# A cross-attention kernel whose order of operations becomes a table, with turned probabilities and rests of queries moved in fewer transfers

## The chip, the cores and the metric

The kernel runs on one core of one Trainium2 chip. A core has the matrix engine (PE, with its weight loads PEld), the vector engine (DVE), the scalar engine (ACT), GpSimd (POOL) and the sync engine (SP), which here issues most DMA transfers. The metric is device time in microseconds (us), from launch to the end of the slowest (here the only) core. Lower is better.

## The reference

Two batches of 2048 image rows of 640 attend over 124 text tokens of 384, with 8 heads of 80. A second path ("adapter") takes the last 4 context tokens, lets rows derived from them attend over all 2048 image rows, turns the result into queries again and lets these attend over the 4 tokens. Both results are added and go through the output matrix, a bias and the residual. All is float32.

```python
enc = encoder_hidden_states[:, :end_pos, :]          # 124 text tokens
ca = encoder_hidden_states[:, end_pos:, :]           # 4 adapter tokens
query = hidden_states @ Wq
keyt = enc @ Wk
valt = enc @ Wv
hs = _mha(query, keyt, valt)
ca_q1 = jnp.einsum('btc,th->bch', ca, Wq_ca)
indices = np.linspace(0, CROSS_ATTENTION_DIM - 1, unet_size).astype(np.int64)
ca_q1 = ca_q1[:, indices, :]
ca_hs1 = _mha(ca_q1, residual, residual)
ca_q2 = ca_hs1 @ Wq
ca_k2 = ca @ Wk_ca
ca_v2 = ca @ Wv_ca
ca_hs2 = _mha(ca_q2, ca_k2, ca_v2)
out = hs + ca_hs2
out = out @ Wout + b_out
out = out + residual
```

`_mha` splits into heads, takes softmax(q k / sqrt(80)) v per head and joins the heads again.

## The kernel before

**A planner issues everything.** The class `Desk` holds five engines and a pseudo engine "NONE". The kernel is written as some sixty generators (tasks); each yields operations (`Do`) that name their engine or a choice of engines, the events that they wait for, the buffers that they need and free (`Room`), and a function that emits the instructions. `run` (line 166) looks at all operations that could start, by the planner's own durations, takes the earliest (ties by rank, by a correction per task from the table `RANKS`, and by `change`, which discourages a change of PE's tile shape), and `issue` (line 182) emits its instructions. `pin` (line 199) holds every instruction to program order, so that each engine runs exactly the sequence that the planner chose. This happens when the program is built; the chip sees five fixed sequences with semaphores between them.

**Blocks and units.** The 4096 image rows are cut into 8 blocks of 512 (0 to 3 the first batch, 4 to 7 the second), and for the text attention into 16 units of 256, each with two tiles of 128 rows.

**Each block.** `x_load` (line 1124) fetches x so that DVE can turn it 32 by 32. `yz_block` (line 1527) multiplies it by small matrices for the adapter (tile shape 64*32: 64 rows and 32 columns of PE). `queries` and `queries_fast` (line 1321) compute Q = x Wq with 128*32 instructions (`by_columns`, line 219: four column groups side by side), the latter by a scheme of seven products for eight (names `wq_sums`, `x_sums`). The queries of 80 columns a head are stored as 64 + 16: the last 16 columns of all heads ("rests") are split by `halves_away` (line 1479) into a rounded half and what is left of it, sent to DRAM, and brought back by `rest_back` (line 1499) in another arrangement, one half block of 256 rows at a time. There `away` writes one transfer for both parts, and four transfers read it back into `landing`, two for each copy.

**The adapter.** `adapter(b)` (line 1646) runs for each batch 24 scores operations whose 128x2048 results DVE reduces to maxima (`mx`), then 24 whose results ACT exponentiates (`ea`); their tile shape is 32*128. All 96 use one PSUM buffer of four banks (the room `quad`), so the next one waits until DVE or ACT has read the last. `contract` (line 1768) multiplies `ea` by `y` (tiles `acc`), and `second` (line 1806) ends the path with a table of 384 rows in DRAM (`o2`).

**Each unit.** `text_scores` (line 1951) computes two tiles of scores (tile shape 64*128; main part and rests). `softmax` (line 1979) reduces, exponentiates, divides (`share`, on POOL, DVE or ACT, as the planner finds them free), turns 32 by 32 (`eb`) and sends the result to DRAM (`kept`). `probabilities` (line 2017) brings a unit's probabilities back, turned, as `pT`: keys on partitions, 32 partitions a transfer, four transfers a unit. `text_out_fast` (line 2171) multiplies them by V (`ph`), copies the results out (`hs`, on ACT or DVE), forms their sums (on DVE or POOL) and runs four `chain`s (line 2226) of products with Wout or sums of it, again seven products for eight; after each step of a chain DVE adds the bank's partial result to rows of x (`x_more`, `last_rows`) before the next step adds to the same bank. `stored` (line 2297) lets POOL gather the adapter's rows onto the sum (`add_second`, line 2127) and stores it; the last unit gathers first and stores by halves (`stored_half`).

**Order of keys.** Key c of a head lies in column c of the scores and of the exponentials, whose last four of 128 columns are zero. The 32-by-32 turns cut the columns into four groups j of 32, and in `pT` key 32 j + b lies on partition 32 j + b: a transfer for each j.

Of the kernel before, what the change touches and what calls it, by code (L numbers as in the profile page):

```python
# [59 lines left out]
class Task:  # L60
    def __init__(self, gen, rank, key, more):
        self.gen, self.rank, self.key, self.more, self.last = gen, rank, key, more, Event()


class Desk:
# [4 lines left out]
    WHOLE, SWITCH, LEAVE, ANOTHER = (P, P), 328.5, 9.9, 185.7  # L70
    START = {(P, P): 0.107, (64, P): 0.143, (P, 64): 0.107, (64, 32): 0.1, (P, 32): 0.03}
    DRAIN = {
        ((P, P), (32, P)): 0.136, ((P, P), (64, P)): 0.035, ((P, P), (P, 64)): 0.056, ((P, P), (P, 32)): 0.067,
        ((32, P), (P, 32)): 0.049, ((P, 64), (P, P)): 0.07, ((P, P), (P, P)): 0.0,
    }
    DRAINS = {(64, P): 0.172, (32, P): 0.108, (P, 32): 0.115}
    MORE = {
        "v_transpose": 0.025, "v_stream_shuffle": 0.09, "v_scalar_tensor_tensor": 0.07, "v_reciprocal": 0.035,
        "a_activation": 0.045,
    }  # L80
    COLD = 5.2
    TAIL = {"PE": 0.25, "DVE": 0.18, "ACT": 0.2, "POOL": 0.25, "SP": 0.1, "NONE": 0.0}


    RANKS = {
        "adapter": {0: 1, 1: 2},
        "chain": {2: 8, 4: -11, 5: 7, 6: -2, 8: -11, 11: -4, 14: 11, 15: 16, 19: -14, 24: -4, 25: 3, 30: 3.1,
            32: 4, 34: 10, 36: 2, 41: 0.5, 42: 1, 43: 0.5, 44: -10, 45: -10, 48: -8, 50: -5, 51: -5, 52: 7,
            54: 10, 55: 10, 56: 10, 68: -4, 76: -3, 81: 2, 86: 2, 87: 3},
        "contract": {0: 5, 1: 4.5, 2: 8, 3: 8},  # L90
        "halves_away": {1: -4, 2: -2, 4: 4, 6: 6},
        "keys": {0: -10},
        "probabilities": {3: -8, 5: -4, 8: 12, 9: -3, 10: -2, 12: 6, 13: 6, 15: 7},
        "queries_fast": {0: 5, 3: 4},
        "rest_back": {1: 11, 4: 5, 7: 8, 9: 9, 10: 5, 14: 2},
        "second": {0: 2.3},
        "softmax": {0: 5, 2: -7, 3: 6.2, 4: -4, 7: -11, 8: 2, 10: -5, 12: -20, 14: -3, 17: 9, 20: -2, 21: 7,
            22: 7, 25: -5, 29: 2, 30: 6},
        "sums_of_wq": {0: 5.7},
        "text_scores": {0: -8, 1: 3.4, 12: 9},  # L100
        "values_weights": {0: -18},
        "x_load": {1: 4.2, 4: 5},
        "y_rows": {2: 2, 3: 6, 4: 4},
        "y_weights": {0: 1},
        "yz_block": {2: 16, 5: 3.5, 6: 5},
    }

    def __init__(self, tc):
        self.tc, self.nc, self.now, self.spent, self.mode = tc, tc.nc, 0.0, 0.0, None
        self.free = {e: 0.0 for e in self.ENGINES}  # L110
        self.queue = {e: [] for e in self.ENGINES}
        self.events, self.landed, self.channel, self.log, self.begun = {}, 0.0, 0.0, [], {}

# [6 lines left out]
    def begin(self, gen, rank):  # L120
        name = gen.__name__
        n = self.begun[name] = self.begun.get(name, -1) + 1
        task = Task(gen, rank, (name, n), self.RANKS.get(name, {}).get(n, 0.0))
        task.last.t = self.now
        self.go_on(task, None)

    def go_on(self, task, value):
        while True:
# [7 lines left out]
        op.task, op.at = task, Event()  # L136
# [5 lines left out]

    def change(self, mode):


        if mode is None or mode == self.mode:
            return 0.0
        return self.LEAVE if self.mode == self.WHOLE else self.SWITCH if mode == self.WHOLE else self.ANOTHER

    def order(self, op):  # L150
        return (op.order() if callable(op.order) else op.order) + op.task.more
# [14 lines left out]
    def run(self):  # L166
# [105 lines left out]
def kernel(  # L272
# [1174 lines left out]

    def front_rooms():

# [940 lines left out]
```

## Time and profile before

| what | value |
|---|---|
| time, median of 3 runs | 581.55 us (581.11 to 582.66) |
| the profiled execution | 581.8 us |
| its span, first to last instruction | 580.1 us |
| granted clock of PE | 1.000 |
| DMA packets | 153039, 112.71 MB |
| SP transfers of `pT<-kept`, of `kept<-eb` | 64, 32 |

The span is what the profile's rows divide up; the run's time has 1.7 us more around it. In rows of groups, the columns after the bar are busy time, the mean of one in ns, and the engine's idle time just before them with what ended it. `128*32` is the tile shape, rows by columns of PE; a float32 product shows as two passes, and by_columns' four groups run side by side, so eight records make one product. A row of the timeline has start, length, engine, line, operation, names and count; in square brackets the idle time before it and what ended it. Nearly all emitting lines are helpers of the planner (L210 `matmul`, L222 `by_columns`, L230 `transpose`, L245 vector, scalar and GpSimd operations, L265 `dma`), so groups are told apart by names. Idle time of an engine that is not the bottleneck costs nothing.

### The profile page before, as it was taken

How to read it: one execution, taken by the hardware profiler on the slowest of the kernel's cores; microseconds unless marked ns; L12 is line 12 of the kernel's file. 1: busy time of each engine (PE TensorE's matmuls, PEld its weight loads, DVE VectorE, ACT ScalarE, POOL GpSimd, SP SyncE). 2: the span in 40 equal slices, each digit the busy share in tenths (PEclk: the TensorE clock that was granted, in tenths of full speed). 3: DMA queues.
4: the chain of work that ended last, by engine and by line, in shares of the span. 5: the costliest groups of instructions: out<-in, count | busy, mean ns of one | idle time of the engine just before them, and what ended most of it. 6: DMA issues, size and time to landing. Idle time of an engine off the chain costs nothing.

```text
span 580.1 us, 19105 instructions
## 1 busy us (share of the span) xinstructions
PE 570.3 (98%) x8115; PEld 308.4 (53%) x8115; DVE 391.7 (68%) x645; ACT 309.8 (53%) x869; POOL 141.6 (24%) x200
## 2 busy tenths in 40 slices
PE   9999999999999999999999999999999999999997
PEld 8885334555555545455455445454455545545453
DVE  2446799999999756356999999973455253444443
ACT  2413376686566898689847447277877613002020
POOL 9102112012206411120114326050140312403241
PEclk9999999999999999999999999999999999999999
DMA  8897866979766888234999969999549487799995
GB/s 245 196 263 131 199 94 187 179 201 172 182 184 137 217 157 221 82 113 149 219 284 247 230 152 236 270 227 275 142 105 266 112 211 155 181 263 247 250 249 139
DMA packets 153039, 112.71 MB, mean 194 GB/s; under 512 B 83701, under 2 KB 126581, under 8 KB 152954
## 3 DMA queue, kind: packets, MB, share of 16 engines
q1 hardware_dynamic: 147322, 100.80, 67.5%
q0 software_dynamic: 5632, 10.69, 11.3%
q8 instruction: 64, 1.05, 0.8%
q14 instruction: 21, 0.17, 0.1%
HBM read 71.23 MB, written 40.22 MB: 192 GB/s over the span
## 4 chain that ended last, share of the span: by engine, by line
PE 64%; DVE 16%; DMA 8%; ACT 6%; issue 4%; SPq 1%; DVEq 0%; ACTq 0%
PE po L222 25%; PE pq L222 9%; PE ph L210 6%; DVE mx L245 6%; PE acc L210 5%; PE s L210 4%; PE pq L210 4%; PE sc L210 3%; ACT ea L245 3%; DMA kept<-eb 3%; DMA pT<-kept 2%; ACT p L245 2%; DVE m L245 2%; DVE q L245 2%; DVE eb L245 2%
## 5 line engine op out<-in xcount | busy, mean ns | idle before, releaser
L245 DVE TENSOR_REDUCE mx<-s 128x4 f32<-128x2048 f32 x48 | 109.4, 2280 | 4.1 <-PE s L210 4.1
L245 ACT ACTIVATE ea<-s 128x2048 f32<-128x2048 f32 x48 | 91.0, 1897 | 24.2 <-PE s L210 23.9
L245 ACT ACTIVATE p<-sc,m 128x124 f32<-128x124 f32 x256 | 90.2, 383 | 10.2 <-DVE m L245 9.7
L222 PE MATMUL po<-wout_sums,hs 128*32 128x320 f32 x1024 | 77.3, 433 | 0.0
L222 PE MATMUL po<-wout_sb,hs 128*32 128x320 f32 x960 | 74.2, 433 | 0.7 <-DVE x_more L245 0.7
L222 PE MATMUL pq<-xt,wq_sb 128*32 128x256 f32 (+1 forms) x928 | 66.3, 418 | 0.5 <-DVE mt L245 0.5
L245 DVE TENSOR_TENSOR x_more<-x_more,po 128x320 f32<-128x320 f32 x72 | 34.3, 483 | 45.5 <-PE po L222 45.4
L2129 POOL DMA_INDIRECT x_more<-o,query x18 | 27.9, 1550 | 124.3 <-DVE x_more L245 92.5
L245 ACT ACTIVATION_READ_ACCUMULATOR p<-sc,m 128x1 f32 x256 | 57.8, 226 | 0.0
L245 ACT COPY hs<-ph 128x512 f32<-128x512 f32 (+1 forms) x34 | 18.5, 551 | 65.8 <-PE ph L210 65.2
L222 PEld LDWEIGHTS po<-wout_sums,hs 128*32 128x32 f32 x1024 | 32.9, 110 | 34.1 <-issue 1.8
L210 PE MATMUL acc<-ea,y_sb 128*32 128x384 f32 (+2 forms) x768 | 51.0, 385 | 0.0
L222 PEld LDWEIGHTS po<-wout_sb,hs 128*32 128x32 f32 x960 | 30.4, 110 | 33.1 <-issue 1.5
L245 DVE TENSOR_REDUCE m<-sc 128x4 f32<-128x496 f32 x64 | 40.0, 662 | 10.4 <-PE sc L210 10.4
L245 DVE TENSOR_TENSOR last_rows<-last_rows,po 128x320 f32<-128x320 f32 x56 | 26.7, 481 | 27.9 <-PE po L222 27.5
L210 PE MATMUL ph<-pT,vpad 128*32 128x256 f32 x768 | 45.3, 380 | 0.1
L245 POOL TENSOR_TENSOR p<-p,r 128x992 f32<-128x992 f32 x8 | 14.8, 1846 | 125.0 <-DVE r L245 125.0
L222 PEld LDWEIGHTS pq<-xt,wq_sb 128*32 128x32 f32 x928 | 27.8, 109 | 29.6 <-issue 13.5
L245 DVE STREAM_TRANSPOSE eb<-p 128x1024 f32<-128x1024 f32 x32 | 39.4, 1233 | 5.6 <-DMA kept<-eb 5.5
L210 PEld LDWEIGHTS sc<-kmain,q 64*128 64x128 f32 x512 | 32.1, 187 | 13.7 <-issue 5.5
L210 PE MATMUL sc<-kmain,q 64*128 64x124 f32 x512 | 38.4, 285 | 0.2 <-ACT p L245 0.2
L245 ACT CAST rests<-landing 128x512 fp32r<-128x512 f32 x30 | 18.7, 635 | 36.2 <-PE sc L210 28.0
(216 smaller groups left out, 847.6 us busy)
## 6 DMA issues: line engine op xcount, KB each, us to landing
kept<-eb SPq DMA_DIRECT2D x32, 512.0 KB, 3.8
pT<-kept SPq DMA_DIRECT2D x64, 256.0 KB, 8.2
landing<-away SPq DMA_DIRECT2D x60, 128.0 KB, 4.3
xi<-in_x_dram SPq DMA_DIRECT2D x56, 128.0 KB, 4.6
x_more<-in_x_dram SPq DMA_DIRECT2D x18, 320.0 KB, 6.8
out_dram<-x_more SPq DMA_DIRECT2D x16, 320.0 KB, 6.6
last_rows<-in_x_dram SPq DMA_DIRECT2D x14, 320.0 KB, 7.2
out_dram<-last_rows SPq DMA_DIRECT2D x14, 320.0 KB, 10.0
```

Source lines behind the costliest of these rows:

```text
L210: self.pin(self.nc.tensor.matmul(out, lhsT, rhs, **kw))
L222: self.pin(self.nc.tensor.matmul(out[j : j + 32], lhsT[:, j : j + 32], rhs, **kw))
L245: self.pin(getattr(engine, what)(*args, **kw))
L2129: desk.pin(nc.gpsimd.indirect_dma_start(out=t, out_offset=None, in_=o2_of[b], in_offset=bass.IndirectOffsetOnAxis(ap=query[:, st : st + 1] ...
```

## The change

**The order.** `RANKS`, `order` and `change` go; in their place stands `TURNS`, which gives each operation of each task (by the task's path in the tree of forks) one number: its place in the whole order is the number's size, its engine the number modulo six. `run` takes operations in that order. Operations whose engine could be chosen get it from the table. The planner's durations are changed too; they no longer decide the order, but still appear in the code.

```diff
+        ".1": [959], ".2": [38, 53, 54, 72, 84, 96, 102, 114, 126, 156, 162, 186, 198, 216, 354, 936], ".3": [362],
...
     def run(self):
+        turn = lambda op: self.TURNS[op.task.path][op.num]
         while any(self.queue.values()):
-            best = None
-            for e in self.ENGINES:
-                found = [(max(r, self.free[e], self.now), op) for op in self.queue[e] if (r := self.ready(op)) is not None]
-                if found:
-                    t = min(x[0] for x in found)
-                    t, op = min(
-                        (x for x in found if x[0] <= t + 1e-9),
-                        key=lambda x: self.order(x[1]) + self.change(x[1].mode),
-                    )
-                    if best is None or t < best[0]:
-                        best = t, e, op
-            assert best, [(e, [(op.order, op.fn.__qualname__) for op in q]) for e, q in self.queue.items()]
-            self.issue(*best)
+            op = min((op for q in self.queue.values() for op in q), key=turn)
+            engine = self.ENGINES[turn(op) % len(self.ENGINES)]
+            self.issue(max(self.ready(op), self.free[engine], self.now), engine, op)
```

**Bookkeeping that follows from it.** Buffers are freed by operations of "NONE" that wait for all their users (`free_x`, `free_q`), where counters decided before; `stored` waits for all sums of a tile by name, always gathers, and has no branch through DRAM; `residual` of the last unit waits for the adapter's table. These emit no instructions.

**Turned probabilities.** Keys take another place in the scores: key 4 k + j lies in column 31 j + k. ACT writes each head's 124 exponentials as four runs of 31 with a zero column after each (`et`), so that after the turns key 4 b + j is row b of group j, and the four transfers of a unit become one over all 128 partitions.

```diff
-        et = e[:, :, :NK]
+        et = e.rearrange("p h (j k) -> p h j k", j=4)[:, :, :, : NK // 4]
...
-                            et[:, h, :], s4[u][:, j, :], AF.Exp, bias=less[u][:, j : j + 1],
+                            et[:, h], s4[u][:, j, :].rearrange("p (j k) -> p j k", j=4), AF.Exp, bias=less[u][:, j : j + 1],
...
-        by_keys = kept.rearrange("(i b) j n -> j b i n", i=4)
+        by_keys = kept.rearrange("(i b) j n -> (b j) i n", i=4)
...
-        for j in range(4):
-            op = yield Do(
-                "SP",
-                lambda: dma(pT[R * j : R * (j + 1)].rearrange("p i k h a -> p i (k h a)"), by_keys[j], 1.1),
-                [("kept", m, 0), ("kept", m, 1)], rank=0,
-            )
+        op = yield Do(
+            "SP", lambda: dma(pT.rearrange("p i k h a -> p i (k h a)"), by_keys, 2.8, 0.38),
+            [("kept", m, 0), ("kept", m, 1)], rank=0,
+        )
...
-                pk3 = pk[:, : B * NTOK].rearrange("p (b t) -> p b t", b=B)[:, :, :NK]
+                pk3 = pk[:, : B * NTOK].rearrange("p (b k j) -> p b j k", b=B, j=4)[:, :, :, : NK // 4]
```

**Rests of queries.** The 16-column rests are laid out so that a row of DRAM holds all four groups of one column. The two parts of a half block go out in a transfer each, as soon as each is there, and come back in one transfer of 4 KB runs, whose source is read twice (a stride of 0). The keys' rests follow the same arrangement once, with four transfers out and one back.

```diff
-        away = away_of[n] = hbm.tile([P, 2, 512], F32, tag=f"rest_{n}", name=f"away_{n}")
+        away = away_of[n] = hbm.tile([2, R, 2, 8 * P], F32, tag=f"rest_{n}", name=f"away_{n}")
...
+            def part_away(i, k=k, z=z):
+                dma(away[k, :, i].rearrange("q (g n) -> q g n", g=4), z[:, i].bitcast(F32), 0.45, 0.45)
...
+            for i, at_i in enumerate((main_at, op.at)):
+                yield Fork(one(Do(
+                    "SP", lambda i=i, part_away=part_away: part_away(i), [at_i], marks=[both_away[i]], rank=0,
+                )), 1)
...
-        for u in range(2):
-            by_rows = away_of[n][VH * u : VH * (u + 1)].rearrange("(g d) i n -> (d i) g n", g=4)
-            for e in range(2):
-                yield Do(
-                    "SP",
-                    lambda u=u, e=e, by_rows=by_rows: dma(
-                        t[VH * u + G * e : VH * u + G * (e + 1)], by_rows[:, :, 2 * P * k : 2 * P * (k + 1)], 0.7
-                    ),
-                    [op.at], marks=[("landed", m, u, e)], rank=0,
-                )
+        by_rows = away_of[n][k].rearrange("q i n -> (q i) n").unsqueeze(1).to_broadcast([2 * R, 2, 8 * P])
+        yield Do(
+            "SP", lambda: dma(t.rearrange("p g n -> p (g n)"), by_rows, 1.45, 0.5), [op.at], marks=[("landed", m)],
+            rank=0,
+        )
```

The columns of the last piece of Wq are put in the matching order (`columns`), and a small mask for the adapter's keys is computed for it on DVE (`own`, three short operations in the front).

More of the change, by code (lines that the diff above doesn't have):

```diff
@@ L80 @@
     }
     COLD = 5.2
[L82 to L105, printed above, removed]
@@ L106 @@
+    TAIL = {"PE": 0.235, "DVE": 0.14, "ACT": 0.145, "POOL": 0.16, "SP": 0.1, "NONE": 0.0}
+    TURNS = {
[204 rows of a table added]
     }
@@ L2133, in add_second @@
         ))
-        desk.spent += 1.9
-        desk.landed = desk.now + desk.spent + 6.5
+        desk.transfer("POOL", 1.7, 1.57)
     def text_out(m):
@@ L2266, in chain @@
-                ends.setdefault((m, i), []).append(op.at)
-                if not tile_left[m, i]:
-                    yield Fork(stored(m, i, ends[m, i]), 1)
+        reads = {(i, u): [] for i in range(2) for u in range(2)}
+        for n, steps in enumerate(chains):
+            for _, _, (place,) in steps:
+                reads[place].append(("sum", m, *place, n))
+        yield Fork(one(Do(
+            "NONE", lambda: None, [("chain", m, n) for n in range(len(chains))], frees=[(hss, at_hs)]
+        )), 0)
```

348 lines of the change are left out of this document (174 added, 174 removed), and 203 rows, old and new, of the table TURNS.

## The prediction

> **What bounds the kernel now.** I read the page first, then the windows, then PE's timeline.
>
> ```profile
> span 580.1 us, 19105 instructions
> ...
> PE 570.3 (98%) x8115; PEld 308.4 (53%) x8115; DVE 391.7 (68%) x645; ACT 309.8 (53%) x869; POOL 141.6 (24%) x200
> ...
> PE 64%; DVE 16%; DMA 8%; ACT 6%; issue 4%; SPq 1%; DVEq 0%; ACTq 0%
> ```
>
> TensorE is busy for 98% of the span. The chain of waits runs for a third of its length over other engines, but that matters only where PE goes idle, and PE is idle for 580.1 − 570.3 = 9.8 us in all. The windows say where.
>
> ```profile
> 0.00:20.00 20.00, 18.86 (x113) 17.03 (x114) 6.73 (x41) 5.39 (x10) 15.57 (x59) 1.00 0.90 274
> ...
> 100.00:150.00 50.00, 49.51 (x756) 26.50 (x748) 49.74 (x65) 33.98 (x133) 11.31 (x9) 1.00 0.90 190
> 150.00:200.00 50.00, 49.48 (x774) 27.30 (x772) 43.87 (x59) 33.46 (x113) 14.59 (x21) 1.00 0.67 170
> 200.00:250.00 50.00, 49.41 (x775) 24.97 (x779) 26.53 (x47) 40.82 (x82) 7.50 (x5) 1.00 0.61 153
> 250.00:300.00 50.00, 48.23 (x745) 27.14 (x733) 39.69 (x57) 40.83 (x120) 7.19 (x6) 1.00 0.73 193
> 300.00:350.00 50.00, 48.96 (x714) 24.29 (x706) 48.87 (x52) 25.43 (x99) 16.56 (x15) 1.00 0.89 216
> ...
> 400.00:450.00 50.00, 49.44 (x787) 25.99 (x779) 23.09 (x39) 38.66 (x69) 7.67 (x6) 1.00 0.70 188
> ...
> 550.00:580.00 30.00, 26.38 (x412) 13.41 (x404) 12.11 (x26) 3.09 (x6) 9.24 (x6) 1.00 0.78 194
> ```
>
> The columns after the length are PE, PEld, DVE, ACT and POOL busy, then the clock (1.00 throughout) and DMA. Idle PE: 1.1 in the first window (before the first product), 3.6 in the last (after the last one), and 0.49 + 0.52 + 0.59 + 1.77 + 1.04 + 0.56 = 5.0 in between. So a new order can win little: the products are the same 8115, and what it can remove is those 5.0 us and time that hides inside "busy" PE. Two such kinds show in the timeline.
>
> ```profile
> 400.63 1.26 PE L222 MATMUL po<-wout_sums,hs 128*32 128x320 f32 x16
> 401.70 0.72 PE L222 MATMUL po<-wout_sb,hs 128*32 128x320 f32 x8
> ...
> 407.51 1.26 PE L222 MATMUL po<-wout_sums,hs 128*32 128x320 f32 x16
> 408.70 0.56 PE L210 MATMUL s<-cop,zop 32*128 32x128 f32 x8
> 409.19 1.07 PE L210 MATMUL acc<-ea,y_sb 128*32 128x256 f32 x16
> ```
>
> Sixteen 320-column instructions, four at a time, take 401.70 − 400.63 = 1.07 us when the next ones use the same tile shape (128*32), and 408.70 − 407.51 = 1.19 when adapter scores (32*128) follow: leaving the 128*32 shape costs 0.12. The other kind is waits:
>
> ```profile
> 272.43 0.56 PE L210 MATMUL s<-cop,zop 32*128 32x128 f32 x8 [0.22 <-ACT ea L245]
> ...
> 273.38 1.88 ACT L245 ACTIVATE ea<-s 128x2048 f32<-128x2048 f32 x1 [1.00 <-PE s L210]
> ...
> 275.31 0.51 PE L210 MATMUL s<-zop,cop 32*128 32x512 f32 x4 [0.46 <-ACT ea L245]
> ...
> 285.38 1.92 PE L222 MATMUL pq<-xt,wq 128*32 128x512 f32 x16
> ...
> 285.47 2.28 DVE L245 TENSOR_REDUCE mx<-s 128x4 f32<-128x2048 f32 x1
> ...
> 287.81 0.51 PE L210 MATMUL s<-zop,cop 32*128 32x512 f32 x4 [0.51 <-DVE mx L245]
> ```
>
> All adapter scores share one PSUM buffer of four banks. From one score operation to the next at least 2.88 us pass (275.31 − 272.43) where ACT reads it, and about 3.2 (0.95 from score to reader, then 2.28) where DVE does; less other work than that between two of them makes PE wait. At 285.47 the reader itself started late, behind other DVE work. A recorded wait is longer than it says: the sixteen 512-column products at 285.38 last 1.07 × 512/320 = 1.71, plus 0.12 for the shape, so the scores could have started at 287.21; the wait was 0.60, not 0.51. With some 20 such waits at 0.1 each, I call the removable waiting 5.0 + 2.0 = 7.0 us.
>
> **The change, part by part. The order.** Both kernels pin each engine's program order; the table gives another one. A table entry modulo six is the engine, its size the place. PE has 550 operations in both, the same set. Sorting the table gives 102 departures from the 128*32 shape, against 107 that I count along PE's timeline; departures from the other shapes differ by one at most. That is 5 × 0.12 = −0.6 us. Next the score spacing. Laying the new PE order out with the durations above (scores 0.49, from 408.70 to 409.19, sixteen product instructions 1.07, and so on), 14 of the 96 score operations come sooner than 2.88 or 3.2 after the one before, against 10 in the old order; the shortfalls add up to 4.1 us in both. One is large: between entries 7092 and 7158 stands a single contraction (two passes of 512 columns, 0.86 at the rate above), which leaves 2.88 − 0.49 − 0.86 − 0.12 = 1.4 us short. Some of the small ones vanish because any earlier wait widens the spacing; I take 1.4 + 1.4 = 2.8 us as left. The waits of the old order that have other causes (a late DVE reader, an accumulating bank whose partial sum is still being read) are those that a recalculated order can remove; by the same layout the steps of one accumulation stand far enough apart everywhere but for 0.3 us in all. So 7.0 − 2.8 = 4.2 us go. Bounds: 0, if as many new ones arise, and all 7.0.
>
> **Who does what.** Softmax's division moves among engines.
>
> ```profile
> L245 DVE TENSOR_REDUCE mx<-s 128x4 f32<-128x2048 f32 x48 | 109.4, 2280 | 4.1 <-PE s L210 4.1
> L245 ACT ACTIVATE p<-p,r 128x124 f32<-128x124 f32 x104 | 31.5, 386 | 8.1 <-DVE r L245 8.1
> L245 POOL TENSOR_TENSOR p<-p,r 128x992 f32<-128x992 f32 x8 | 14.8, 1846 | 125.0 <-DVE r L245 125.0
> L245 DVE TENSOR_TENSOR p<-p,r 128x992 f32<-128x992 f32 x11 | 13.6, 1239 | 0.3
> L245 ACT COPY hs<-ph 128x512 f32<-128x512 f32 (+1 forms) x34 | 18.5, 551 | 65.8 <-PE ph L210 65.2
> ```
>
> Of 32 divisions, 8 ran on POOL, 11 on DVE and 104/8 = 13 on ACT; the table puts 20, 3 and 9 there. DVE is relieved of 8 × 1.24 = 9.9 us, but takes 14 more of the copies `hs<-ph` (5 before, 19 now; 0.55 each on ACT, about 8 us), so its 391.7 us stay. POOL takes 12 × 1.85 = 22 us more on 141.6. The result is needed a transfer and many us later, so the slower POOL costs nothing; without that cover it would cost 0.6 each. The activations write the same 124 elements in four runs instead of one; I take 0, and were each 10% slower, ACT (53% busy) would still cover it.
>
> **The transfers.** The turned probabilities come back in one transfer a unit instead of four; the rests of a half block go out in two instead of one and come back in one instead of four.
>
> ```profile
> kept<-eb SPq DMA_DIRECT2D x32, 512.0 KB, 3.8
> pT<-kept SPq DMA_DIRECT2D x64, 256.0 KB, 8.2
> landing<-away SPq DMA_DIRECT2D x60, 128.0 KB, 4.3
> ...
> 309.54 1.84 SPq L265 DMA_DIRECT2D pT<-kept  x4
> ...
> 532.59 5.80 SPq L265 DMA_DIRECT2D pT<-kept  x4
> ```
>
> SP issues 64 − 16 = 48 transfers fewer for the probabilities and 64 + 16 − 16 − 32 = 32 fewer for the rests, at 1.84/4 = 0.46 each some 37 us of its queue; SP is not on PE's path, so this wins nothing by itself. The bytes stay. What matters is whether one transfer of 4 × 256 KB lands before its products. Bounds for its landing: 3.8, what half of it takes as `kept<-eb`, and 14.0, the 5.8 over which one unit's four issues stretched (at 532.59) plus 8.2. I take 8.2, the quarter's median while its siblings are in flight, as the sixteen engines carry the same bytes. In the table the work on PE between that issue and the unit's first product is 8.0 us in the tightest unit (the third; entries 8536 to 8796), then 10.6, 11.7, 11.8, 12.9, and 14 or more in the other eleven. So +0.2 us; at 14.0 it would be 6.0 + 3.4 + 2.3 + 2.2 + 1.1 = 15.0. The rests' single transfer replaces quarters that landed in 4.3, with 4 KB runs instead of 1 KB; 0.
>
> **The ends.** The front keeps its idle 1.1 us and the same loads. The tail:
>
> ```profile
> 567.52 1.54 POOL L2129 DMA_INDIRECT last_rows<-o,query  x1 [0.61 <-DVE last_rows L245]
> ...
> 575.66 0.72 PE L222 MATMUL po<-wout_sb,wout_sums 128*32 128x320 f32 x8
> ...
> 576.45 0.49 DVE L245 TENSOR_TENSOR x_more<-x_more,po 128x320 f32<-128x320 f32 x1 [1.13 <-PE po L222]
> ...
> 576.97 0.33 SPq L265 DMA_DIRECT2D out_dram<-x_more  x1
> ```
>
> After the last product come one addition, one store and its landing, 580.1 − 576.4 = 3.7 us, in both. The last gather-add started 8.9 us before PE's end; in the table 8.6 us of products follow it, and its store stands ahead of the last two half stores on SP's queue, where a late landing would hold them: 0, at most +1.
>
> **The sum.** The profiled execution took 581.8 us, 1.7 beyond its span and 0.25 above the median of the runs. Against the median: 581.55 − 0.6 − 4.2 + 0.2 = 577.0.
>
> **The rivals.** (1) *Nothing is won.* PE is full in both, and the order before was also laid out by a planner; the new one meets other waits of the same size, since DVE is as full (49.74 of 50 in the window 100 to 150) and the score shortfall is equal. Against it: the waits found had causes that an order can avoid. Time: 581.55 − 0.6 = 581.0, no change that can be told. (2) *The single transfer is late: slower.* Landing later than about 12.1 us, its waits (4.1 + 1.5 + 0.4 + 0.3 = 6.3) push 577.0 over 583.3. For it: DMA reads 0.89 and 0.90 busy in two of the windows above, and PE's queue is in order, so one late unit holds everything. Against it: the four, issued within 1.84 at 309.54, took only about 1.84 + 8.2 = 10 in all. With a landing of 13: 5.0 + 2.4 + 1.3 + 1.2 + 0.1 = 10.0, so 587. (3) *POOL's divisions hold DVE.* If each of 12 more divisions kept DVE from its own two-input work for 1.85 us, DVE would gain 22 − 9.9 = 12 us in stretches where it is the fullest engine; half of it on PE's path gives 583. Against it: PE lost only 0.49 us in the window where DVE was busy for 49.74 of 50. The Trainium skill (GPSIMD Engine Reference, Key points) speaks for this one: GpSimd shares its SBUF interfaces with VectorE, contends with instructions of two SBUF inputs, and VectorE does elementwise work about twice as fast. The trace has 1.85 against 1.24 for the division, 1.5 times; whether it held DVE, the group rows do not show.
>
> **How the numbers follow.** Forecast 0.66 (its own range 572.5 to 579.8), rival 1 0.17, rival 2 0.12, rival 3 0.05. About 0.3%, 1.7 us, is what a measurement of this kernel can tell from no change: faster means under 579.8, slower over 583.3. So faster 0.66, same 0.17, slower 0.17. The low end is all 7.0 us gone and the shortfall absorbed, with a little from the tail: 581.55 − 0.6 − 7.0 = 574.0, and 2.5 more for waits that hide deeper in busy PE than I count: 571.5. The high end takes in rival 3 and the near half of rival 2: 585.
>
> **What would show it.** PE's idle time in the windows between 20 and 550 falls from 5.0 us to about 2, with a wait of some 1.4 us on ACT's `ea` just before the last scores of the first batch. The `pT` row shows 16 issues of 1024 KB landing in about 8 us, and no `ph` product names a DMA as what ended its wait; if one does, rival 2 is at work. POOL's `p<-p,r` stands at x20. Rival 3 would show as DVE idle on "issue" and additions of one SBUF pair growing beyond their length. PE's busy time falling by more than 1 us, or a wait over 3 us anywhere, would contradict the account.

## The result: no change that can be told, and the profile after

| kernel | median us (runs) | lowest to highest | standard deviation |
|---|---|---|---|
| before | 581.76 (17) | 580.62 to 582.66 | 0.5 |
| changed | 581.10 (17) | 579.02 to 583.88 | 1.3 |

The ratio is 0.9988, 95% interval 0.9975 to 1.0001. The forecast was 577.0, with 571.5 to 585.0 as its range; the time is that of rival 1 (581.0). The runs of the changed kernel scatter more than twice as much, which no part of the prediction had looked at.

The page of the changed kernel first, its rows as in the prediction.

```profile
span 579.8 us, 18971 instructions
...
PE 566.5 (98%) x8115; PEld 308.3 (53%) x8115; DVE 390.7 (67%) x663; ACT 290.9 (50%) x813; POOL 160.3 (28%) x213
...
L425 POOL TENSOR_TENSOR p<-p,r 128x992 f32<-128x992 f32 x20 | 38.9, 1943 | 169.7 <-DVE r L425 148.8
...
L425 DVE TENSOR_TENSOR x_more<-x_more,po 128x320 f32<-128x320 f32 x64 | 30.5, 482 | 37.6 <-PE po L403 37.3
...
kept<-eb SPq DMA_DIRECT2D x32, 512.0 KB, 4.6
pT<-kept SPq DMA_DIRECT2D x16, 1024.0 KB, 7.6
landing<-away SPq DMA_DIRECT2D x15, 512.0 KB, 4.8
```

The same products take PE 3.8 us less (570.3 before), yet the span shrinks by 0.3. The rest is idle time, so the windows come next (PE, PEld, DVE, ACT, POOL, clock, DMA share, GB/s).

```profile
0.00:20.00 20.00, 18.27 (x107) 16.66 (x108) 7.68 (x34) 3.94 (x7) 15.40 (x59) 1.00 0.86 270
...
100.00:150.00 50.00, 49.24 (x756) 26.21 (x752) 49.67 (x61) 30.23 (x111) 13.78 (x10) 1.00 0.69 157
...
250.00:300.00 50.00, 48.82 (x798) 29.22 (x802) 41.03 (x60) 42.78 (x134) 7.84 (x6) 1.00 0.51 168
...
320.00:340.00 20.00, 19.00 (x289) 10.52 (x284) 18.17 (x23) 14.59 (x57) 0.74 (x1) 1.00 1.02 335
340.00:360.00 20.00, 19.08 (x272) 9.71 (x268) 17.63 (x25) 6.84 (x34) 9.50 (x7) 1.00 0.76 225
...
550.00:580.00 30.00, 22.75 (x340) 10.62 (x332) 11.50 (x26) 0.00 (x0) 13.32 (x9) 0.96 0.80 187
...
565.00:574.00 9.00, 9.00 (x136) 4.16 (x128) 3.08 (x7) 0.00 (x0) 2.82 (x2) 1.00 0.92 245
```

PE is idle for 0.76 + 1.18 + 1.00 + 0.92 us in the four stretches between 100 and 360, and with the rest of the windows for 4.5 us between 20 and 550, against 5.0 before. More is lost outside. In the first 20 us PE idles for 1.73 us, against 1.14 before; the second profile of the same kernel (e1) has 1.13 there, so this loss comes in some runs and not in others. Behind 550 us stands a wait of 1.38 where the old order had none. The rows of that wait and of the end, by PE's timeline:

```profile
555.08 1.28 PE L403 MATMUL po<-wout_sums,hs 128*32 128x320 f32 x16 [1.38 <-POOL hs L425]
...
572.87 1.26 PE L403 MATMUL po<-wout_sb,hs 128*32 128x320 f32 x16
```

It ends at 572.87 + 1.26 = 574.13, where the old order ended at 575.66 + 0.72 = 576.38. So PE is done 2.2 us earlier, but the tail from there to the end of the span grew from 3.7 to 5.7 us. Together these are −3.8 in busy PE, −0.5 + 1.4 in its waits, +1.9 in the tail and +0.6 in the front: −0.4, near the 0.3 by which the spans differ. DMA is at its fullest in one of the stretches where PE idles: share 1.02 and 335 GB/s from 320 to 340. In the stretches from 100 and from 250 its share is only 0.69 and 0.51, so not every wait goes with transfers. The windows of the kernel before for the same two places:

```profile
320.00:340.00 20.00, 19.65 (x280) 9.19 (x276) 19.80 (x23) 7.82 (x33) 4.69 (x7) 1.00 1.04 235
565.00:575.00 10.00, 10.00 (x156) 4.95 (x152) 4.16 (x10) 0.00 (x0) 3.08 (x2) 1.00 0.57 126
```

DMA's share is as high there, but its rate is lower and PE loses 0.35 instead of 1.00; at the end the share is 0.57 instead of 0.92. What PE waited for, in the list of waits (total, times, longest):

```profile
PE po L403 <- POOL hs L425: 2.3, 2, 1.4
PE s L394 <- ACT ea L425: 1.2, 2, 1.0
PE unread L394 <- DVE zeros L425: 1.1, 1, 1.1
PE ph L394 <- DMA pT<-kept: 1.0, 1, 1.0
```

POOL's timeline around the two waits on `hs`, and DVE's longest wait for a landing before `eb`:

```profile
327.25 1.25 DVE L425 STREAM_TRANSPOSE eb<-p 128x1024 f32<-128x1024 f32 x1 [0.67 <-DMA kept<-eb]
...
345.42 2.43 POOL L425 TENSOR_TENSOR p<-p,r 128x992 f32<-128x992 f32 x1
347.22 2.12 POOL L425 TENSOR_TENSOR hs<-hs 128x256 f32<-128x256 f32 x2
...
550.87 1.55 POOL L2323 DMA_INDIRECT last_rows<-o,query  x1 [12.40 <-DMA last_rows<-in_x_dram]
552.73 1.55 POOL L2323 DMA_INDIRECT x_more<-o,query  x1 [0.31 <-issue]
553.70 1.33 POOL L425 TENSOR_TENSOR hs<-hs 128x256 f32<-128x256 f32 x1
```

A sum that a chain needs stands on POOL behind a division (345.42) and, near the end, behind two gathers that waited for a load. And DVE's turn into the only buffer `eb` (327.25) needs the store before it to have landed.

### The profile page after: what moved, and what is told of

The parts are those of the page before. It is cut to its first block, busy times and chain, and to the rows that moved or that the text cites. A ratio compares the mean times of both kernels' runs of the same rounds, so it can differ in the third digit from the quotient of the medians.

```text
span 579.8 us, 18971 instructions
## 1 busy us (share of the span) xinstructions
PE 566.5 (98%) x8115; PEld 308.3 (53%) x8115; DVE 390.7 (67%) x663; ACT 290.9 (50%) x813; POOL 160.3 (28%) x213
## 4 chain that ended last, share of the span: by engine, by line
PE 75%; DMA 7%; DVE 7%; SPq 4%; ACT 2%; issue 2%; POOL 2%; DVEq 0%; ACTq 0%; POOLq 0%
PE po L403 23%; PE pq L403 19%; PE acc L394 7%; PE sc L394 6%; PE ph L394 6%; PE s L394 6%; PE pq L394 3%; SPq L445 3%; DVE mx L425 2%; DMA last_rows<-in_x_dram 2%; PE pyz L394 2%; DMA last_rows<-o,query 2%; DVE xt L425 1%; DMA xi<-in_x_dram 1%; ACT ea L425 1%
## 5 line engine op out<-in xcount | busy, mean ns | idle before, releaser
L425 POOL TENSOR_TENSOR p<-p,r 128x992 f32<-128x992 f32 x20 | 38.9, 1943 | 169.7 <-DVE r L425 148.8
L403 PE MATMUL po<-wout_sums,hs 128*32 128x320 f32 x1024 | 78.7, 433 | 1.4 <-POOL hs L425 1.4
L403 PE MATMUL po<-wout_sb,hs 128*32 128x320 f32 x928 | 72.1, 434 | 1.0 <-POOL hs L425 0.9
L425 DVE TENSOR_TENSOR last_rows<-last_rows,po 128x320 f32<-128x320 f32 x64 | 30.3, 482 | 46.9 <-PE po L403 46.7
L425 ACT ACTIVATION_READ_ACCUMULATOR p<-sc,m 128x1 f32 x256 | 56.4, 220 | 0.0
L425 DVE TENSOR_TENSOR x_more<-x_more,po 128x320 f32<-128x320 f32 x64 | 30.5, 482 | 37.6 <-PE po L403 37.3
L394 PE MATMUL ph<-pT,vpad 128*32 128x256 f32 x768 | 48.0, 380 | 1.0 <-DMA pT<-kept 1.0
L425 POOL TENSOR_TENSOR hs<-hs 128x256 f32<-128x256 f32 x29 | 27.2, 1029 | 71.1 <-ACT hs L425 31.2
L425 ACT COPY hs<-ph 128x512 f32<-128x512 f32 (+1 forms) x24 | 13.6, 573 | 54.2 <-PE ph L394 54.1
L2323 POOL DMA_INDIRECT x_more<-o,query x16 | 25.5, 1593 | 53.0 <-DVE x_more L425 45.5
```

The source lines that it names most:

```text
L394: self.pin(self.nc.tensor.matmul(out, lhsT, rhs, **kw))
L403: self.pin(self.nc.tensor.matmul(out[j : j + 32], lhsT[:, j : j + 32], rhs, **kw))
L425: self.pin(getattr(engine, what)(*args, **kw))
L2323: desk.pin(nc.gpsimd.indirect_dma_start(out=t, out_offset=None, in_=o2_of[b], in_offset=bass.IndirectOffsetOnAxis(ap=query[:, st : st + 1] ...
```

## The experiments

All times are medians; the ratio is to the kernel before, run on the same chip, with its 95% interval. Edits of the order change single entries of the table: task, operation, old place, new place. Tails are measured from the end of PE's last row; the expectations count from the start of the last product, 0.45 us earlier.

**e1, the changed kernel again.**

> The changed kernel once more, unaltered, for a second profile of it. Theory A (the new order removes old waits and makes new ones at fixed places): the same places come back, each within 0.4 us: 1.6 us at unit 8's product before the last gathers' sums (POOL hs), 1.2 at unit 2's first product (DMA pT<-kept), 1.1 before the last scores of the first batch (ACT ea), 1.1 at unit 2's last chain (POOL hs), and 5 to 6 us between PE's end and the last landing; time 581.1. Theory B (the waits are spread at random by DMA landings): other places, the same sum of 4 to 5 us.

Measured: 580.9 (579.33 to 583.45), 0.9979 (0.9966 to 0.9992). Three waits came back at their places (`ea` 1.03, `pT` 1.17, `hs` of unit 2 0.92), so theory A holds for them. The one before the last gathers' sums, expected at 1.6, was 0.47. And in this profile another stands at 378, and behind it a store that took 11.4 us to land (timeline of SP, DVE and PE):

```profile
364.54 0.52 SPq L445 DMA_DIRECT2D kept<-eb  x1
...
376.05 1.25 DVE L425 STREAM_TRANSPOSE eb<-p 128x1024 f32<-128x1024 f32 x1 [1.67 <-DMA kept<-eb]
...
378.12 1.28 PE L403 MATMUL po<-wout_sums,hs 128*32 128x320 f32 x16 [0.71 <-DVE x_more L425]
```

DVE, in order, held an addition to `x_more` behind the turn, and PE waited for the addition. Part of the waiting is a matter of landings, not of places alone.

**e2, new order with four transfers a unit; e3, old order with one.**

```diff
-            "SP", lambda: dma(pT.rearrange("p i k h a -> p i (k h a)"), by_keys, 2.8, 0.38),
+            "SP", lambda: [
+                dma(pT[R * j : R * (j + 1)].rearrange("p i k h a -> p i (k h a)"), by_keys[R * j : R * (j + 1)], 1.1)
+                for j in range(4)
+            ],
```

e3 takes the key layout of the change into the kernel before; its first operation of four issues the whole transfer, the other three nothing.

> The changed kernel with its order, but each unit's turned probabilities come back in four transfers of 32 partitions, issued one behind the other at the place of the single one. Theory A (the order decides): SP's queue is 16 x 1.4 = 22 us busier and the wait at unit 2's first product stays at 1 to 2.5 us; time 581 to 583. Theory C (the single transfer costs what the order won): the DMA wait goes and the time falls by 1.2 us or more, to 580 or less.

> The kernel before with its own order on every engine, instruction for instruction, but with one transfer a unit for the turned probabilities, at the place of the first of the four (keys placed as in the changed kernel). Theory A: within 0.5 us of before, 581.8, since PE's order is the same and its waits are not on these transfers. Theory C: 583 or more, with products ph that wait on DMA pT<-kept. If the shorter queue of SP is worth anything by itself it shows here, as 581 or less.

Measured: e2 591.03, 1.0162 (1.0141 to 1.0183), ten us slower than the changed kernel, which neither theory allowed. e3 581.46, 0.9989 (0.9981 to 0.9998), some 0.7 faster than before. So theory C is wrong both ways round: the single transfer costs neither order anything, and the new order cannot do without it. The 0.7 is as much as the whole change won in the first measurement (0.66). In e2, unit 2's product waited for 4.2 us, as PE's timeline shows:

```profile
337.37 1.94 PE L394 MATMUL ph<-pT,vpad 128*32 128x256 f32 x16 [4.18 <-DMA pT<-kept]
```

The clock fell while PE still waited, and stayed low behind the wait, as e2's windows show (clock third from the end).

```profile
330.00:337.40 7.40, 3.19 (x52) 2.08 (x49) 5.39 (x5) 2.94 (x10) 0.00 (x0) 0.81 1.05 285
337.40:341.00 3.60, 3.60 (x32) 1.75 (x36) 1.89 (x3) 1.58 (x8) 0.74 (x1) 0.50 0.95 266
```

At half the clock the sixteen 256-column instructions above took 1.94 us instead of the 1.07 of the `acc` row in the prediction. Between 20 and 550 PE idles for 10.9 us here, and is busy for 570.3: both rose.

**e4, two waits on POOL taken away.**

```diff
+for path, n, old, new in (
+    ('.71.1', 2, 13215, 13293),
+    ('.71.1', 3, 13245, 13299),
+    ('.58.3.6', 0, 9123, 9122),
+    ('.58.3.7', 0, 9147, 9128),
+):
+    assert Desk.TURNS[path][n] == old
+    Desk.TURNS[path][n] = new
```

> The changed kernel with two sums of unit 2 on DVE instead of POOL and the first two gathers of the last unit behind unit 8's last sum on POOL. Theory A: the two waits on POOL hs (1.6 at 555 us and 1.1 at 349 us) go and nothing takes their place: 581.1 - 2.7 = 578.4. Theory B: the time moves by less than 1 us, and waits of the same size stand elsewhere.

Measured: 581.31 (579.77 to 584.35), 0.9990 (0.9976 to 1.0004): theory B's time. The two waits are gone, and others stand in their place (PE's timeline of e4):

```profile
330.27 0.74 PE L403 MATMUL po<-wout_sb,hs 128*32 128x320 f32 x8 [1.04 <-DVE x_more L425]
335.78 1.07 PE L394 MATMUL ph<-pT,vpad 128*32 128x256 f32 x16 [1.74 <-DMA pT<-kept]
```

The window around them:

```profile
320.00:340.00 20.00, 17.18 (x257) 9.27 (x249) 16.02 (x22) 12.71 (x51) 0.74 (x1) 1.00 0.94 288
```

PE loses 2.8 us here, where the changed kernel's first profile lost 1.0. Both waits lie ahead of the place that was edited, where this kernel's order is that of the changed one. So the edit did not make them. The row at 335.78 names a landing; the one at 330.27 stands behind a turn into `eb` that started 2.20 us late, and that a landing held it is not shown. A profile of one run cannot price an edit here.

**e5 to e8, single places.** e5 moved unit 8's last store behind the last half stores and a chain step of the last unit behind one of unit 8; e6 fetched unit 2's probabilities two places earlier; e7 moved the last adapter scores of the first batch behind the text scores, to fill the 1.4 us that the prediction had found short; e8 has all these and e4's.

```diff
+    ('.64.3.9', 2, 13678, 13732),
+    ('.71.3.13', 0, 13392, 13518),
+    ('.71.3.13', 1, 13454, 13526),
...
+    ('.58.3', 2, 8536, 8506),
+    ('.54.8.1', 0, 8506, 8512),
+    ('.60.1', 1, 8512, 8518),
...
+    ('.55', 108, 7158, 7206),
+    ('.55', 109, 7189, 7207),
+    ('.55.1', 3, 7236, 7290),
+    ('.55.1', 4, 7280, 7292),
+    ('.55.1', 5, 7374, 7428),
+    ('.55.1', 6, 7412, 7436),
```

> The changed kernel with unit 8's gathered store issued behind the last half stores on SP's queue, and one chain step of the last unit behind one of unit 8, on PE and DVE, so that unit 8's last gather starts earlier. Theory A (the order's gain of 2.2 us at PE's end is given back in the tail, 5.7 us from the last product's start to the end of the span against 3.5 to 4.2 before): the tail falls to 4.2 to 4.6 and the time by 1.1 to 1.6, from 581.0 to 579.6. Theory B (the end is set by how many stores are in flight, whatever their order): within 0.5 us of 581.0.

> The changed kernel with unit 2's turned probabilities fetched two places earlier on SP's queue, ahead of one store of x_sums and one of probabilities. Theory A: the wait at unit 2's first product (1.2 and 1.35 us in two profiles) goes, time 579.8. Theory D (the stretch from 320 to 340 us is full of transfers: DMA share 1.00 to 1.02 there in both profiles): what is passed lands later by as much, and the wait stands again at 0.7 us or more, there or at an addition of x_more; time 580.5 to 581.3.

> The changed kernel with the last adapter scores of the first batch behind the text scores that followed them, and the first two of the second batch behind products of queries, on PE, ACT and DVE alike. Theory A: the wait of 1.1 us on ACT's ea at 275 us goes, at most one more change of shape (0.1) comes: 580.0 if it reaches the end. Theory D: PE only runs earlier into the full stretch of transfers behind it, which ends when it ended before: 580.8 to 581.2, with 1 us more waiting between 320 and 400.

> The edits of the four kernels that move single places, together (sums and gathers off POOL's queue, the tail, the earlier transfer of unit 2, the adapter's scores). Theory A: 581.0 - 1.4 - 1.2 - 1.0 - 1.5 = 576 to 577.5, if each stands by itself; the POOL edit alone gave nothing, so without it 577.5 to 578.5. Theory D: only the tail and what lies behind 400 us counts, 579 to 580.

Measured: e5 581.11, 0.9987 (0.9974 to 0.9999). e6 581.94, 0.9996 (0.9979 to 1.0013), in two groups, six runs from 579.76 to 581.01 and six from 582.86 to 583.9. e7 588.42, 1.0103 (1.0077 to 1.0129). e8 588.84, 1.0105 (1.0085 to 1.0124). No edit won anything that can be told, and e7 and e8 lost some 7 us, which no theory allowed. e5's tail was 4.7 us, shorter than in the first two profiles, and its time is theory B's all the same. In e7 the last scores feed exponentials that the contraction behind them needs, so the wait moved there and grew (PE's timeline):

```profile
280.81 1.35 PE L394 MATMUL acc<-ea,y_sb 128*32 128x128 f32 x16 [2.04 <-ACT ea L425]
```

and the clock fell behind it, as e7's windows show:

```profile
282.00:284.00 2.00, 1.97 (x24) 0.89 (x24) 0.00 (x0) 2.00 (x13) 0.00 (x0) 0.50 0.57 222
```

In all PE idles for 9.7 us between 20 and 550 in e7 and is busy for 569.2, against 4.5 and 566.5.

**e9 and e10, fewer transfers in the full stretch.** Both kernels without the same stores; in the old one the order is kept on every engine.

```diff
+            if m in (11, 12, 13):
+                desk.spent += 0.45
+                return
...
+        kept = kept_of[9 if m in (11, 12, 13) else m].rearrange("p j k n -> p j (k n)")
```

> The changed kernel without the stores of the turned probabilities of units 11 to 13, which read unit 9's again: 512 KB less at 314, 320, 328 and 336 us, and the next turn on DVE (one buffer eb) no longer waits for such a store to land. Theory D (the new order puts these transfers so close that the stretch from 320 to 400 is paced by their landings, more or less by chance from run to run): DVE's waits for a landing before eb (0.67 and 0.28 in one profile, 2.20 and 0.95 in the slowest) vanish, PE loses less than 1 us between 320 and 340 instead of 1.0 to 2.8, the time falls to 579 to 579.6 and the runs spread as before's do (standard deviation 0.5 instead of 1.2 to 1.5). Theory A (fixed places of the order alone): 580.7 or more, with the spread unchanged.

> The kernel before with the same stores left out, its order kept, as a control. Theory D: its stores stand 12 us and more apart where DMA is full, so nothing waits for them: 581.7 to 582.2, within 0.5 of before, spread as before's. If any order gains from less to transfer, 580.5 or less.

Measured: e9 579.89, 0.9956 (0.9944 to 0.9968), standard deviation 0.7. e10 582.36, 0.9998 (0.9987 to 1.0009). Against its own chip's before, e9 is 2.5 us faster, the changed kernel 0.7 and 1.35 faster than its own. The stores cost the new order some 1.2 to 1.9 us and the old one nothing; the interval of e9 is clear of the first measurement's and just touches e1's (0.9966 to 0.9992). DVE's waits before `eb` vanished from 300 us on (two earlier ones, at 193 and 218, stayed). Of PE's loss between 320 and 340, 0.9 us stayed:

```profile
320.00:340.00 20.00, 19.08 (x292) 10.54 (x286) 18.50 (x24) 14.59 (x57) 0.73 (x1) 1.00 0.89 267
```

That is a wait on `pT` (0.92), so theory D's time came, with only part of its waits. The edit removes bytes and, with them, the landings that later turns and fetches of the three units wait for; it does not tell the two apart. The old order is not free of such waits either. Its stores from 364 to 394 follow each other by 8.3 to 10.7 us, not 12; in the profile of the prediction a turn into `eb` waits 5.00 us for a landing (404.88), and PE 0.53 for the addition behind it (406.94).

**e11, the last gathers left out.**

```diff
-        op = yield Do("POOL", lambda: add_second(t, b, st), [*both, ("o2", b), "query"])
+        op = yield Do("POOL", lambda: add_second(t, b, st) if m != 8 else None, [*both, ("o2", b), "query"])
```

> The changed kernel without the gather-adds of unit 8's two tiles (the adapter's rows are left out there), their stores in place. Theory A (the tail is held by gathers, which crowd the last 15 us, and by the store that waits for the last of them on SP's queue): from the last product's start to the end of the span 4.2 to 4.6 us instead of 5.2 to 6.1, and the time 579.6 to 580.0. Theory B (it is the stores themselves): tail 5.2 or more, time 581.

Measured: 579.69, 0.9955 (0.9942 to 0.9968). The tail is 576.5 − (571.02 + 1.26) = 4.2 us (4.7 by the expectation's measure), from the last row of PE's timeline:

```profile
571.02 1.26 PE L403 MATMUL po<-wout_sb,hs 128*32 128x320 f32 x16
```

DMA's share there is 0.55, close to the old order's 0.57, where the changed kernel has 0.92. The window of e11:

```profile
565.00:573.00 8.00, 7.28 (x110) 3.25 (x100) 3.24 (x7) 0.00 (x0) 0.00 (x0) 1.00 0.55 207
```

The gathers hold the tail and fill DMA there: the thirteen profiles from e1 to e16 that keep them in the new order have tails of 4.7 to 6.1 us. PE also ends 1.85 us earlier in this profile than in the first. That part is not shown to be the edit's: the two gathers left out stood at 564.73 and 566.58, behind POOL's last sum (553.70), and this is the profile of the fastest of five runs (578.33).

**e12 to e16, versions that compute everything.** e12 joins e5 and e6 and puts one turn into `eb` behind an addition. e13 adds a second buffer for the turn, e14 only moves unit 8's last store to the end of SP's queue, e15 joins both with e4's two sums of unit 2 on DVE, e16 adds e6's fetch. The core of e13:

```diff
+            late["yt"] = pool.tile([P, 2, 512], F32, name="yt")
...
-                t = late["pool"].tile([P, 512], F32, tag=f"yt{z[0]}", name=f"yt_{b}_{sb}_{u}")
+                t = late["yt"][:, z[0]]
...
+                if len(stored_y) == 2 * len(blocks):
+                    ebs.at.append(0.0)
...
+        if i:
+            return late["yt"].rearrange("p u n -> p (u n)").rearrange("p (j h a) -> p j h a", j=4, h=HEADS)
```

> The changed kernel with the earlier fetch for unit 2, the tail's edit, and one turn of probabilities (eb) behind the addition to x_more that stood behind it on DVE. Theory D: the addition no longer waits for a landing, so the late group of runs (582.8 to 583.9 with the earlier fetch alone) goes or thins out; 580 to 580.5. Theory A: as the single edits, 581 to 581.5, still in two groups.

> The changed kernel, every engine's order and all transfers kept, with a second buffer for the turned probabilities (eb) from 271 us on, in the place of yt, which is no longer used then. Theory D with the buffer as its cause: no turn on DVE waits for a landing between 300 and 400 us; the late group of runs (582 to 584) goes, standard deviation 0.7 or less instead of 1.2 to 1.3, and the median falls from 581.0 to 580.0 to 580.4. If the landings of pT and x_more are the cause: 581 with the same spread.

> The changed kernel with nothing but unit 8's last store behind the last two half stores on SP's queue. Theory A: the half stores go out 1 to 1.5 us earlier, from the last product's start to the end of the span 4.8 to 5.3 us instead of 5.6 to 6.1, time 580.3. Theory B: the store that is now last ends as late as the half stores did: 581.0.

> Second eb buffer, unit 8's last store last, and two sums of unit 2 on DVE instead of POOL. If the gains add up: 581.0 - 0.8 - 0.7 - 0.8 = 578.7, spread 0.7. If the stretch after 320 takes back what comes earlier: 580.

> The same as the one before it and the earlier fetch for unit 2. If its wait of 1.2 us on pT goes without another in its place: 577.7 to 578.2; if what is passed on SP's queue lands later by as much (as with the earlier fetch alone, where the median rose by 0.9): 579 or more.

Measured: e12 582.22, 0.9997 (0.9980 to 1.0014), still in two groups. e13 580.65, 0.9977 (0.9964 to 0.9990), standard deviation 1.0, two of twelve runs late (582.69, 582.87). e14 581.36, 0.9980 (0.9969 to 0.9991). e15 581.97, 0.9992 (0.9978 to 1.0006). e16 581.70, 0.9990 (0.9978 to 1.0002). In e13 no turn waits for a landing from 271 us on, where the second buffer begins, and still the time moves by less than its interval: the buffer is not the cause by itself. e14's tail stayed at 5.7 us, so the order of the last stores is not what makes it long. In e15 unit 2's product waited 1.95 us for `pT` (PE's timeline):

```profile
335.06 1.93 PE L394 MATMUL ph<-pT,vpad 128*32 128x256 f32 x16 [1.95 <-DMA pT<-kept]
```

The clock halved behind it, by e15's windows:

```profile
332.00:335.00 3.00, 1.11 (x20) 0.42 (x16) 3.00 (x3) 0.99 (x4) 0.00 (x0) 1.00 1.05 386
335.00:338.00 3.00, 2.94 (x28) 1.54 (x32) 1.95 (x4) 0.89 (x4) 0.23 (x1) 0.50 1.06 384
```

None of these is faster than the changed kernel beyond the intervals.

**e17 and e18, both places cleared in both kernels** (the edits of e9 and e11 together; in the old kernel the last two gathers and the same stores, its order kept).

> The changed kernel without the stores of the turned probabilities of units 11 to 13 (which read unit 9's again) and without the gather-adds of unit 8's two tiles. If the two places are separate and hold the lost gain: 0.9956 - 0.0025 = 0.993 of before, 578.2, spread 0.6, and PE ends 3 us and more earlier than in before. If they share one cause (the gain of the one is taken back at the other): 579.5 to 580.

> The kernel before, its order kept, with the same two left out. If only the new order suffers from them: 582.0 to 582.3, within 0.3 of before (its tail is at 4.2 us already). If gathers at the end cost in any order: 581 or less.

Measured: e17 577.38, 0.9936 (0.9914 to 0.9957); e18 581.96, 0.9993 (0.9984 to 1.0002). Ten of e17's twelve runs lie between 576.71 and 578.75, two at 582.03 and 583.21. With both sets of transfers out, the new order is 577.38 − 581.96 = 4.6 us faster than the old one with the same left out; by the ratios, which the two late runs weigh on, it is (0.9993 − 0.9936) × 582.27 = 3.3. The page of e17:

```profile
PE 566.6 (99%) x8115; PEld 308.6 (54%) x8115; DVE 390.6 (68%) x663; ACT 290.4 (51%) x813; POOL 156.9 (27%) x211
```

Its windows:

```profile
320.00:340.00 20.00, 20.00 (x304) 10.88 (x298) 18.94 (x25) 14.75 (x57) 1.66 (x2) 1.00 0.87 270
340.00:360.00 20.00, 20.00 (x288) 9.97 (x286) 18.93 (x26) 6.47 (x33) 8.44 (x7) 1.00 0.72 204
```

And its last row of PE:

```profile
569.35 1.26 PE L403 MATMUL po<-wout_sb,hs 128*32 128x320 f32 x16
```

The last row of PE in e18:

```profile
576.01 0.72 PE L222 MATMUL po<-wout_sb,wout_sums 128*32 128x320 f32 x8
```

PE does the same 8115 products in the same busy time as in the changed kernel (566.6 and 566.5), loses nothing from 320 to 360, and ends at 570.61. That is 3.5 us earlier than there, and 6.1 earlier than in e18 (576.73); its tail (574.8 − 570.6 = 4.2) is 1.4 shorter than the changed kernel's. Between 20 us and its end PE idles for 2.9 us.

## Why the prediction was wrong

**The order: a gain near the forecast size is there, but not in the kernel's time.** The prediction gave −0.6 for departures and −4.2 for waits, −4.8 in all. e17 against e18 shows −4.6 (−3.3 by the ratios) with the two sets of transfers left out. That difference contains the change's transfers too, and the single transfer alone was worth some 0.7 in the old order (e3), so the order's own part is not measured alone. e17's 2.9 us of idle PE is near the 2.8 that the prediction left. The part inside "busy" PE is there: 570.3 us before, 566.5 in the first profile, 566.6 in e17, 567.5 in e1, though the prediction's last paragraph said that more than 1 us would contradict it. That sentence was at odds with its own 0.6 + 2.0 hidden. Counted along the records of the traces, departures from 128*32 fall from 120 to 112, by 8 and not 5: at 0.12 each that is 1.0 us, an estimate. That the rest of the 2.8 to 3.8 is short waits is not shown. More hidden time went than the 2.6 that was forecast.

**The step that failed is the bound on the new waits.** I took 2.8 us as left, from score spacing alone: the new order was laid out engine against engine with the transfers as if they landed whenever needed. They were priced one at a time (slack of one fetch against one landing time) and never summed over a stretch. In the changed kernel PE still loses 4.5 us between 20 and 550 and 1.4 behind it, 5.9 in all, where "about 2" was to be seen. Of the 4.5, 1.9 lie between 320 and 360, which begins with DMA at 335 GB/s; in e4's profile it is 3.6 there (17.18 and 19.21 busy of 20.00 each). There e9 shows the cost, some 1.2 to 1.9 us, and e10 that the old order does not pay it. Whether it is the bytes in one stretch or the landings that engines wait for, the runs leave open. The 1.4 behind 550 (0.47 in e1) is a wait for a sum on POOL, which the prediction did not price: it weighed POOL's divisions, not the sums that stand behind them and behind gathers on its queue.

**The single transfer: landing right, its place wrong.** 8.2 us was assumed; the page says 7.6. The products of the tightest unit were to have 0.2 us of wait; one wait after `pT` takes 1.0 in the first profile, 1.2 in e1 and 1.95 in e15. In the first profile (timelines of SP and PE):

```profile
325.82 0.43 SPq L445 DMA_DIRECT2D pT<-kept  x1
...
333.86 1.07 PE L394 MATMUL ph<-pT,vpad 128*32 128x256 f32 x16 [1.00 <-DMA pT<-kept]
```

The product starts 8.0 us after the issue, as the 8.2 would have it. But PE was there after 7.0 us, not 8.0: SP issued the fetch later against PE's work than the table's places let expect. And "SP is not on PE's path, so this wins nothing" is off by some 0.7 us in the old order (e3) and by far in the new one, where the four transfers cost 10 us (e2). Rival 2 was the reverse of the truth: not that the single transfer slows, but that the order would have been 10 us slower without it.

**The tail: 0, at most +1, was wrong; it is +1.9** (5.7 against 3.7; e1 has 5.1). I named the store that stands ahead of the last half stores; e14 moves it and the tail stays. The last gather also started only 574.13 − 566.58 = 7.6 us before PE's end, not 8.6:

```profile
566.58 1.55 POOL L2323 DMA_INDIRECT last_rows<-o,query  x1 [0.30 <-issue]
```

e11 and e17 show that the last two gathers make it: without them 4.2 in both. How much of that is their traffic and how much the stores that wait for them, the runs do not separate.

**The predicted score wait** came where it was said, 1.03 us before the last scores of the first batch (forecast 1.4). e7 moved the scores and did not fill it: it is a chain through ACT, and the wait came behind the scores instead.

**Rival 1** had the time and half a reason: new waits of the same size, but not because the order was worth nothing. **Rival 3** is not seen. POOL does 20 divisions at 1.94 us each, and DVE's additions take 482 ns, 483 before. (DVE took 13 copies `hs<-ph`, not the 19 that the prediction counted; its busy time stayed as forecast.) PE does wait 2.3 us for POOL's sums, behind a division once; e4 takes both waits away and wins nothing that can be measured.

**Still open:** the late runs. e13 thins them out, e17 still has two, and whether `pT` or the loads of `x_more` start them was not settled. Runs of 583 and more are profiled twice, e4 (584.35) and e15 (583.00): in both, unit 2's product waits longest for `pT`, 1.74 and 1.95 us, where the other profiles but e2's and e7's have 1.2 or less. That this wait starts a late run is a guess from two profiles.

## What to carry to other kernels

When a new order is priced, lay out the transfers on the same time axis as the products and sum their bytes over each stretch of 10 or 20 us. Here an order that removed waits between engines pulled transfers together (335 GB/s from 320 to 340, where the old order had 235), and its gain showed in the time only when some transfers were left out. A scatter of runs that grows (here from 0.5 to 1.3 us) says that an order now hangs on landings; an edit is then priced by the median of ten runs and a control in the old order, not by the wait that one profile shows. To find where an expected gain went, leave the suspected transfers out of both kernels: what only the new one gains is the answer. It says which transfers, and not yet whether their bytes or the waits for their landing are what costs.

## What the runs showed of the hardware

**The clock fell after some waits of about 2 us and not after others.** A wait of 1.95 us (e15) was followed by a granted clock of 0.50, and so was one of 2.04 (e7); each time the clock stayed there for 3.4 us, until 338.4 and 284.9. In e2 it was at 0.50 from 334.6, inside the wait of 4.18 us, to 341.4. But in the same run two more waits, of 2.13 and 1.94 us, left it at 1.00. The row of the first of these and the window around it:

```profile
369.40 1.07 PE L394 MATMUL ph<-pT,vpad 128*32 128x256 f32 x16 [2.13 <-DMA pT<-kept]
360.00:380.00 20.00, 17.87 (x276) 9.78 (x276) 16.49 (x23) 8.48 (x37) 9.05 (x6) 1.00 0.98 216
```

A wait of 1.74 us (e4) left it at 1.00 too, and in e8 it fell at 301.2 behind two waits of only 0.89 and 0.69. So the length of a wait alone does not decide, and what does, these runs do not show. A stretch of 3.4 us at half the clock costs some 1.7 us on top of the wait (an estimate: half of it). The Trainium skill (TensorE: Matmul & The Clock Gate, The two states you'll see) says that the clock goes to half after at least one idle window of about 3.4 us; in e15 and e7 the trace has it after less.

**Landing times stretch threefold.** The same 512 KB store `kept<-eb` landed in 3.2 us at best and 11.4 at worst within one run. The row is the tile's own view in e1's profile:

```profile
DMA to landing us min/median/max: 3.2/4.6/11.4
```
